# Scheduling a layer-norm, convolution and graph layer by stated latencies: pieces that name their time behind them, separate streams for rows and finishes

## The chip, the cores and the metric

One core of a Trainium2 chip. The metric is the device time of one execution in microseconds (us): the median of the runs, lower is better. The runs of one kernel differ by up to 0.55%, most of them by less. The experiments were taken on three chips, with the kernel before beside them each time (medians 2696.2 to 2699.8), so small differences between experiments are safer read from the ratios. A ratio is computed as the mean time of one kernel's fast runs over that of the other's of the same rounds, so it is not quite the ratio of the medians quoted.

## The reference

32 batches of a 512 x 256 matrix. A layer norm and relu give `h`. Three things are made from `h` and meet in a GRU-like gate:

```python
h = jnp.maximum(layernorm(x), 0.0)                  # per batch 512 x 256
# 1: convolution branch (channels first)
c = relu(bn1(conv1d(h, conv1_w, pad 0)))            # "rows" below: a 1-tap convolution
c = bn2(conv1d(c, conv2_w, pad 8))                  # 17 taps
x_conv = relu(c + h)
# 2: graph branch
s = h @ w_se.T + b_se                               # 3 columns
A = exp(-(squared distances of s)) * adj            # 512 x 512, from memory
x_nmp = A @ relu(h @ w_msg.T + b_msg)
# 3: gates
gi = concat(x_conv, x_nmp) @ w_ih.T + b_ih
gh = h @ w_hh.T + b_hh
r, z = sigmoid(gi_r + gh_r), sigmoid(gi_z + gh_z)
out = x + (1 - z) * tanh(gi_n + r * gh_n) + z * h
```

All arithmetic is f32.

## The kernel before

Batches go in groups of four. The 17-tap convolution is done by a nested fast algorithm: 25 products a group (called taps in places), whose input combinations ("operands") and output combinations ("sums") are VectorE and ScalarE work. An evacuation is the operation of another engine that reads a finished sum out of its buffer in PSUM, where TensorE writes its sums, and so frees the buffer. The kernel's author writes the issue order by hand: Python generators yield between pieces of TensorE work, and a loop decides which generator goes on. What is issued on one engine runs there in that order.

The pieces of one batch (cut):

```python
def begin(b):                       # transpose the normalized x: h
    for d in range(ND):
        norm_t(b, d)
        yield 0.55                  # TensorE us of the piece just issued
    if b + 2 < B:
        load(b + 2)                 # x_sb has two buffers
        NORMS[b + 2] = norm(b + 2)  # statistics: VectorE, issued bit by bit by pace()

def rows(b): ...                    # conv1: two pieces of 1.73
def graph(b):                       # messages, factors, exp, masks, gather
    for c in range(NT):
        messages(b, msg, c)
        if c == NT - 1:
            factors()               # VectorE
        yield 0.93
    factors_t(); yield 0.67
    kernel_exp(at); yield 1.2
    for n in range(NT):
        masked(b, at, n); yield 0.55
    for d in range(ND):
        yield from gather(b, msg, at, d)
```

The gates of a batch (cut); the last batch's finish (transposes of `o_sb`, whose last writer is GpSimd) stands inside them:

```python
for o in range(ND):
    yield from products(ps_r, o, 0, 0, 1)      # hidden part, 2 matmuls
    if o == 0:
        while b not in evacuated:
            SUMS.pop(0)[0]()                   # sums and xconv evacuations, ScalarE
        nc.vector.tensor_tensor(xconv, xconv, hT, op=ALU.add)
        nc.scalar.activation(xconv, xconv, AF.Relu)
        yield from finish_waiting()            # finish of the batch before
    yield from products(ps_r, o, 0, 1, 3)
    nc.scalar.activation(r, ps_r, AF.Sigmoid, ...)   # issued on the turn after the yield
    ...                                        # h, z, n likewise, then tanh and three GpSimd ops
```

The choice of the next generator goes by share of work done, and knows nothing of what is ready:

```python
def stage_one(g):
    for b in new:
        yield from begin(b)
        yield from graph(b)
    yield "rows wanted"             # convolution alone until the operands of the group are read
    for b in new:
        yield from rows(b)
...
streams["one"] = [stage_one(g + 1), 77.0 * 0.86, 0.0]
streams["three"] = [stage_three(g - 1), 130.0, 6.0]      # gates
streams["conv"] = [conv, 82.5 * 0.96, 0.0]
while streams:
    step(min(streams, key=lambda k: streams[k][2] / streams[k][1]))
```

Of the kernel before, what the change touches and what calls it, by code (L numbers as in the profile page):

```python
# [2 lines left out]

# [11 lines left out]
P = 128  # L15
# [10 lines left out]
_COL = {}  # L26
_NCOL = 0
for _n, _w in _VECS:
    _COL[_n] = _NCOL
    _NCOL += _w  # L30
G = 4
U = 57
V = U + 2
# [8 lines left out]
def kernel(  # L42
# [400 lines left out]
    def convolution():  # L443

        nonlocal at_product
        wg = (w for _ in range(NG) for w in weights_again())
        for g in range(NG):
            sums = summed(g)
            next(sums)
            done = None  # L450
            for n in range(25):
                at_product = m = 25 * g + n
                while len(WS) < min(m + 1 + AHEAD_W, 25 * NG):
                    WS.append(next(wg))
                while len(X2) < m + 1:
                    while operand_some() is None:
                        yield "rows", g
                w, x2 = WS[m], X2[m].rearrange("p (r v) -> p r v", v=V)
                ps = cps.tile([P, NZ], F32, name="ps_c")
                for o in range(ND):  # L460
                    matmul_sum(
                        ps[:, o * NU : (o + 1) * NU].rearrange("p (b u) -> p b u", u=U),
                        [
                            (w[:, k, i, o * P : (o + 1) * P], x2[:, i * G : (i + 1) * G, k : k + U])
                            for k in range(2)
                            for i in range(ND)
                        ],
                    )
                    if o == 0 and done is not None:
                        sums.send(done)  # L470
                    yield "pe", 1.65
                WS[m] = X2[m] = None
                done = ps
            sums.send(done)
            yield "group", g


    def late_pools():
# [89 lines left out]
            XR[b, c] = late.tile([P, 2, D], F32, name="y", bufs=2)  # L568
            nc.sync.dma_start(XR[b, c], x[b].rearrange("(c p) d -> p c d", p=P)[:, c : c + 2, :])

    waiting = []

    def finish_waiting():
        while waiting:
            for c in range(0, NT, 2):
                finish(*waiting[0], c)
                yield 0.55
            waiting.pop(0)

    def begin(b):  # L580

        for d in range(ND):
            norm_t(b, d)
            yield 0.55
        if b + 2 < B:
            load(b + 2)
            NORMS[b + 2] = norm(b + 2)

    def rows(b):
        nonlocal made  # L590
# [6 lines left out]
    def graph(b):  # L597

        msg = front.tile([P, NT, D], F32, name="msg", bufs=1)
        at = front.tile([P, NT, N], F32, name="at", bufs=1)  # L600
        for c in range(NT):
            messages(b, msg, c)
            if c == NT - 1:
                factors()
            yield 0.93
        factors_t()
        yield 0.67
        kernel_exp(at)
        yield 1.2
        for n in range(NT):  # L610
            masked(b, at, n)
            yield 0.55
        for d in range(ND):
            yield from gather(b, msg, at, d)

    def gates(b):
# [8 lines left out]
        def cols(o, g):  # L625
            return slice(g * D + o * P, g * D + (o + 1) * P)

        def products(ps, o, g, first, last):

            parts = [(whh, 0, hT[:, 0, :], hT[:, 1, :])]  # L630
            parts += [(wih, 0, *x_in[:2]), (wih, ND, *x_in[2:])] if x_in else [None, None]
            for k in range(first, last):
                w, at, *rhs = parts[k]
                for i in range(ND):
                    nc.tensor.matmul(  # L635
                        ps, w[:, at + i, cols(o, g)], rhs[i],
                        start=(k == first_of and i == 0), stop=(k == last_of and i == ND - 1),
                    )
                yield 1.73

        for o in range(ND):
            ps_r = acc.tile([P, N], F32, name="ps_acc")
            first_of, last_of = 0, 2
            yield from products(ps_r, o, 0, 0, 1)
            if o == 0:
                while b not in evacuated:
                    SUMS.pop(0)[0]()
                xconv = XC.pop(b)[:, :, :N]
                nc.vector.tensor_tensor(xconv, xconv, hT, op=ALU.add)  # L649
                nc.scalar.activation(xconv, xconv, AF.Relu)  # L650
                x_in = [xconv[:, i, :] for i in range(ND)] + [XN[b, d] for d in range(ND)]
                yield from finish_waiting()
            yield from products(ps_r, o, 0, 1, 3)
            r = late.tile([P, N], F32, name="r", bufs=2)
            nc.scalar.activation(r, ps_r, AF.Sigmoid, bias=brz[:, o : o + 1])  # L655
            ps_h = acc.tile([P, N], F32, name="ps_acc")
            first_of, last_of = 0, 0
            yield from products(ps_h, o, 2, 0, 1)

            nc.vector.scalar_tensor_tensor(  # L660
                r, ps_h, vec[:, _COL["b_hh"] + 2 * ND + o : _COL["b_hh"] + 2 * ND + o + 1], r,
                op0=ALU.add, op1=ALU.mult,
            )
            ps_z = acc.tile([P, N], F32, name="ps_acc")
            first_of, last_of = 0, 2
            yield from products(ps_z, o, 1, 0, 3)
            z = late.tile([P, N], F32, name="z")
            nc.scalar.activation(z, ps_z, AF.Sigmoid, bias=brz[:, ND + o : ND + o + 1])
            if o == 0:
                load_gates(b + 1)  # L670
            ps_n = acc.tile([P, N], F32, name="ps_acc")
            first_of, last_of = 1, 2
            yield from products(ps_n, o, 2, 1, 3)
            nc.vector.tensor_tensor(r, ps_n, r, op=ALU.add)  # L674
            nc.scalar.activation(  # L675
                r, r, AF.Tanh,
                bias=vec[:, _COL["b_ih"] + 2 * ND + o : _COL["b_ih"] + 2 * ND + o + 1],
            )

            t = o_sb[:, o, :]  # L680
            nc.gpsimd.tensor_tensor(t, hT[:, o, :], r, op=ALU.subtract)  # L681
            nc.gpsimd.tensor_tensor(t, z, t, op=ALU.mult)  # L682
            nc.gpsimd.tensor_tensor(t, r, t, op=ALU.add)  # L683
        load_res(b)
        load_sums(b + 1, 0)
        load_sums(b + 1, 1)
        waiting.append((b, o_sb))


    bn1_sc, bn1_sh = bn_affine("bn1")  # L690
# [40 lines left out]
                break  # L731
            credit -= 0.06 + 0.0011 * size

    def stage_one(g):

        new = range(g * G, (g + 1) * G)
        for b in new:
            yield from begin(b)
            yield from graph(b)
        yield "rows wanted"  # L740
        for b in new:
            yield from rows(b)

    def stage_one_first():


        def to_rows(b):
            yield from begin(b)
            yield from rows(b)

        yield from to_rows(0)
        for b in range(G):
            between = to_rows(b + 1) if b + 1 < G else iter(())
            for k, got in enumerate(graph(b)):
                yield got
                if k >= 3:
                    yield from islice(between, 1)

    def stage_three(g):
        for b in range(g * G, (g + 1) * G):  # L760
            yield from gates(b)

# [5 lines left out]
        for c in range(ND):  # L768
            nc.sync.dma_start(wflat[:, c, k0:k1, :], conv2_w[:, c, k0:k1, :])

    for got in stage_one_first():
        pace(got, 1.2)
    while prepare_next():
        pass

    conv = convolution()
    for g in range(NG):

        streams = {}
        if g + 1 < NG:  # L780
            streams["one"] = [stage_one(g + 1), 77.0 * 0.86, 0.0]
        if g > 0:
            streams["three"] = [stage_three(g - 1), 130.0, 6.0]
        streams["conv"] = [conv, 82.5 * 0.96, 0.0]
        rate = 0.4 if g > 0 else 0.7

        def step(name):

            stream = streams[name]
            got = next(stream[0], None)  # L790
            if got is None:
                del streams[name]
            elif got == "rows wanted":
                while freed < g:
                    step("conv")
            elif isinstance(got, tuple):
                kind, value = got
                if kind == "pe":
                    stream[2] += value
                    pace(value, rate)  # L800
                elif kind == "rows":
                    step("one")
                elif kind == "group":
                    del streams[name]
            else:
                stream[2] += got
                pace(got, rate)

        while streams:
            step(min(streams, key=lambda k: streams[k][2] / streams[k][1]))  # L810
    for got in stage_three(NG - 1):
        pace(got, 1.0)
    for _ in finish_waiting():
        pass


# [47 lines left out]
```

## Time and profile before

| | before |
|---|---|
| median, us | 2698.68 (2693.2 to 2703.8) |
| TensorE busy, granted clock | 89%, 0.935 |
| TensorE idle | 306 us |
| VectorE, ScalarE, GpSimd busy | 44%, 24%, 13% |
| DMA queue's share of 16 engines | 29.9% |

In the profile, L-numbers are lines of the kernel; "A <- B" in a wait is "A could not start until B ended". In a timeline row the two first numbers are start and length in us, and the bracket is the idle time of the engine just before. PE is TensorE, DVE VectorE, ACT ScalarE, POOL GpSimd, SPq the queue from which all DMA is issued. Of the names, `msg` and `aug` are the messages and the three columns of `s`, evacuated from one buffer; `augl` is made of `aug` for the factors; `veps` is a step of the layer norm's statistics; `y <- ps_tr` is the last addition of a finish.

### The profile page before, as it was taken

The numbers are of one execution on the slowest core, as the hardware profiler recorded it, in microseconds if no ns is written. First come the engines' busy times: TensorE is split into PE (matmuls) and PEld (weight loads), VectorE is DVE, ScalarE is ACT, GpSimd is POOL, SyncE is SP. The second block draws the span as 40 slices with busy tenths as digits, with TensorE's granted clock in tenths as the row PEclk, the third lists the DMA queues.
The fourth block names the chain that finished last, engine by engine and source line by source line (L and its number), as shares of the span: only waits on it lengthen the run. The fifth ranks groups of instructions, "written<-read, shape, count | busy, mean of one in ns | idle before, by whom it ended". The sixth has DMA issues, their size and how long they took to land.

```text
span 2695.4 us, 21705 instructions
## 1 busy us (share of the span) xinstructions
PE 2389.5 (89%) x8224; PEld 1493.0 (55%) x8224; DVE 1187.6 (44%) x1989; ACT 637.8 (24%) x930; POOL 337.4 (13%) x239
## 2 busy tenths in 40 slices
PE   5678878999799997999989998999979999999887
PEld 3347655655456654656556665555545565666443
DVE  5655625442455424554155443454435432544211
ACT  3322122222321213222132222322232221311211
POOL 1000001111011100111101101011101101121122
PEclk8779889999899998999999999999999999999899
DMA  5444333332233322333223332323223232232111
GB/s 206 171 144 152 121 118 102 117 106 90 67 113 110 110 101 77 111 109 110 87 77 106 117 117 71 105 102 110 102 74 113 94 108 76 79 114 88 55 63 31
DMA packets 132279, 277.87 MB, mean 103 GB/s; under 512 B 11984, under 2 KB 61520, under 8 KB 131536
## 3 DMA queue, kind: packets, MB, share of 16 engines
q1 hardware_dynamic: 132176, 276.50, 29.9%
q8 instruction: 65, 1.06, 0.2%
q14 instruction: 38, 0.31, 0.0%
HBM read 213.01 MB, written 63.44 MB: 103 GB/s over the span
## 4 chain that ended last, share of the span: by engine, by line
PE 78%; DVE 6%; ACT 4%; POOL 3%; issue 2%; DMA 1%; POOLq 0%; SPq 0%; DVEq 0%; ACTq 0%
PE ps_acc L635 36%; PE ps_c L92 21%; PE ps_g L545 8%; PE ps_g L92 7%; ACT xconv L412 2%; PE ps_tr L536 2%; POOL o_sb L681 1%; PE ps_tr L559 1%; PE ps_g L525 1%; PE ps_tr L217 1%; POOL o_sb L682 1%; DVE at L538 1%; DVE xconv L649 1%; POOL o_sb L683 1%; DMA x_sb<-in_x_dram 1%
## 5 line engine op out<-in xcount | busy, mean ns | idle before, releaser
L92 PE MATMUL ps_c<-x,w 128*128 128x228 f32 x3200 | 720.1, 370 | 45.1 <-issue 39.1
L92 PEld LDWEIGHTS ps_c<-x,w 128*128 128x128 f32 x3200 | 626.5, 199 | 209.5 <-issue 181.8
L635 PE MATMUL ps_acc<-xconv,wih 128*128 128x512 f32 x768 | 390.5, 634 | 40.7 <-ACT xconv L650 40.7
L635 PE MATMUL ps_acc<-hTb,whh 128*128 128x512 f32 x768 | 367.6, 607 | 25.9 <-ACT r L655 25.9
L635 PE MATMUL ps_acc<-xnb,wih 128*128 128x512 f32 x768 | 362.5, 594 | 0.0
L681 POOL TENSOR_TENSOR o_sb<-hTb,r 128x512 f32<-128x512 f32 x64 | 97.1, 1517 | 1575.8 <-ACT r L675 1575.8
L545 PE MATMUL ps_g<-at,msg 128*128 128x512 f32 x512 | 248.9, 614 | 21.4 <-DVE at L538 20.5
L635 PEld LDWEIGHTS ps_acc<-xconv,wih 128*128 128x128 f32 x768 | 153.0, 205 | 186.7 <-issue 140.6
L635 PEld LDWEIGHTS ps_acc<-hTb,whh 128*128 128x128 f32 x768 | 144.6, 193 | 155.5 <-issue 123.0
L635 PEld LDWEIGHTS ps_acc<-xnb,wih 128*128 128x128 f32 x768 | 144.9, 191 | 137.7 <-issue 136.4
L674 DVE TENSOR_TENSOR r<-ps_acc,r 128x512 f32<-128x512 f32 x64 | 44.1, 689 | 314.9 <-PE ps_acc L635 314.9
L545 PEld LDWEIGHTS ps_g<-at,msg 128*128 128x128 f32 x512 | 98.3, 195 | 123.0 <-issue 95.0
L238 DVE TENSOR_TENSOR x<-x 128x471 f32<-128x471 f32 x200 | 165.6, 839 | 0.6
L492 DVE TENSOR_TENSOR msg<-ps_g,bmsg 128x256 f32<-128x256 f32 x128 | 54.0, 423 | 249.2 <-PE ps_g L92 249.2
L538 DVE TENSOR_TENSOR at<-ps_tr,at 128x512 f32<-128x512 f32 x128 | 86.1, 687 | 170.6 <-PE ps_tr L536 170.5
L241 DVE SCALAR_TENSOR_TENSOR x<-x,x 128x471 f32<-128x471 f32 (+1 forms) x184 | 153.8, 836 | 2.3
L92 PE MATMUL ps_g<-wmsg,hT 128*128 128x259 f32 x512 | 139.8, 400 | 16.4 <-DVE aug L493 14.3
L551 ACT ACTIVATE xnmp<-ps_g 128x512 f32<-128x512 f32 x64 | 38.2, 597 | 454.1 <-PE ps_g L545 348.8
L559 PE MATMUL ps_tr<-ident,o_sb 128*128 128x128 f32 x256 | 53.9, 344 | 90.6 <-POOL o_sb L683 83.0
L147 POOL TENSOR_TENSOR rstd<-veps,mhalf 128x4 f32<-128x4 f32 x32 | 38.2, 1194 | 762.7 <-DVE veps L146 762.5
L92 PEld LDWEIGHTS ps_g<-wmsg,hT 128*128 128x128 f32 x512 | 99.1, 199 | 61.5 <-issue 44.4
L660 DVE SCALAR_TENSOR_TENSOR r<-ps_acc,vec,r 128x512 f32<-128x512 f32 x64 | 47.9, 748 | 192.8 <-PE ps_acc L635 192.8
(97 smaller groups left out, 2182.6 us busy)
## 6 DMA issues: line engine op xcount, KB each, us to landing
w<-wd SPq DMA_DIRECT2D x200, 512.0 KB, 3.5
m_sb<-in_adj_dram SPq DMA_DIRECT2D x128, 256.0 KB, 2.7
x_sb<-in_x_dram SPq DMA_DIRECT2D x32, 512.0 KB, 4.9
hd<-hT SPq DMA_DIRECT2D x32, 512.0 KB, 3.0
nd<-xnmp SPq DMA_DIRECT2D x64, 256.0 KB, 2.1
hTb<-hd SPq DMA_DIRECT2D x32, 512.0 KB, 4.1
xnb<-nd SPq DMA_DIRECT2D x64, 256.0 KB, 3.3
y<-in_x_dram SPq DMA_DIRECT2D x64, 256.0 KB, 4.0
```

The lines of the kernel that those rows point to most:

```text
L92: nc.tensor.matmul(ps, lhsT, rhs, start=(i == 0), stop=(i == len(pairs) - 1))
L238: nc.vector.tensor_tensor(dst, get(a), get(b), op=ALU.subtract)
L241: nc.vector.scalar_tensor_tensor(dst, a, -2.0, b, op0=ALU.mult, op1=ALU.add)
L412: nc.scalar.activation(XC[b][:, o, :].rearrange("p (u e f) -> p f e u", e=3, f=3), y[:, :, :, c : c + U], AF.Identity, bias=bn2_sh[:, o : ...
L492: nc.vector.tensor_tensor(msg[:, c, :], ps[:, :D], bmsg[:, :D], op=ALU.add)
L536: nc.tensor.transpose(ps[:, c, :], m[:, c * P : (c + 1) * P], ident)
L538: nc.vector.tensor_tensor(part, ps, part, op=ALU.mult)
L545: nc.tensor.matmul(ps, msg[:, c, d * P : (d + 1) * P], at[:, c, :], start=(c == 0), stop=(c == NT - 1))
L559: nc.tensor.transpose(ps[:, j, d * P : (d + 1) * P], o_sb[:, d, (c + j) * P : (c + j + 1) * P], ident)
L635: nc.tensor.matmul(ps, w[:, at + i, cols(o, g)], rhs[i], start=(k == first_of and i == 0), stop=(k == last_of and i == ND - 1),)
L660: nc.vector.scalar_tensor_tensor(r, ps_h, vec[:, _COL["b_hh"] + 2 * ND + o : _COL["b_hh"] + 2 * ND + o + 1], r, op0=ALU.add, op1=ALU.mult,)
L681: nc.gpsimd.tensor_tensor(t, hT[:, o, :], r, op=ALU.subtract)
```

## The change

The intent: let every piece say how long other engines need before its stream can go on, let the loop skip streams whose time has not come, make rows and finishes streams of their own, and issue each gate evacuation with the last matmul of its sum. No arithmetic, tile or buffer is altered. The core of the diff (cuts marked "...", comments added, the `if` lines before the last streams left out):

```diff
+    def run(streams, rate):
+        now = 0.0
+        ready = {name: 0.0 for name in streams}
+        hold = {name: HOLD.get(name) for name in streams}
+        while set(streams) - {"finish"}:
+            names = [k for k in streams if hold[k] is None or hold[k]()]
+            able = [k for k in names if ready[k] <= now]
+            if able:
+                name = min(able, key=lambda k: streams[k][2] / streams[k][1])
+            else:
+                name = min(names, key=lambda k: ready[k])
+                now = max(now, ready[name])
...
+                pe, after = got if isinstance(got, tuple) else (got, 0.0)
+                now += pe
+                ready[name] = now + after
...
             if c == NT - 1:
                 factors()
-            yield 0.93
+            yield 0.93, 0.0 if c < NT - 1 else 4.5
         factors_t()
-        yield 0.67
+        yield 0.67, 3.0
         kernel_exp(at)
-        yield 1.2
+        yield 1.2, 5.5
         for n in range(NT):
             masked(b, at, n)
-            yield 0.55
+            yield 0.55, 1.0 if n < NT - 1 else 2.5
...
+                if k == last - 1 and then is not None:
+                    then()                      # the evacuation, with the sum
+                yield 1.73, after               # 5.0 behind the residual
...
+    def all_finishes():
+        for b in range(B):
+            yield lambda: b in unfinished
+            yield 0.0, 10.0
+            for c in range(0, NT, 2):
+                finish(b, unfinished[b], c)
+                yield 0.55
...
+        streams = {"conv": [conv, 85.5 * 0.96, 0.0], "finish": [finishes, 1e9, 0.0]}
+            streams["graphs"] = [all_graphs(g + 1), 63.0 * 0.8, 0.0]
+            streams["rows"] = [all_rows(g + 1), 14.0, 9.0]
+            streams["gates"] = [all_gates(g - 1), 129.0, 6.0]
```

## The prediction

> **What bounds the kernel now.** I read the page first, then the engines' busy time by stage, then TensorE's waits in one repeating group, then its timeline at the start of that group. The page:
>
> ```profile
> PE 2389.5 (89%) x8224; PEld 1493.0 (55%) x8224; DVE 1187.6 (44%) x1989; ACT 637.8 (24%) x930; POOL 337.4 (13%) x239
> PE   5678878999799997999989998999979999999887
> PEclk8779889999899998999999999999999999999899
> PE 78%; DVE 6%; ACT 4%; POOL 3%; issue 2%; DMA 1%; POOLq 0%; SPq 0%; DVEq 0%; ACTq 0%
> ```
>
> TensorE is the only engine near full, and 78% of the chain that ended last is its work. But 89% is not 100%: 2695.4 - 2389.5 = 306 us idle, and the clock row falls under 9 where the busy row does. By stage (columns: window, its length, busy us of PE, PEld, DVE, ACT, POOL, granted clock, DMA share, GB/s):
>
> ```profile
> 0.00:172.00 172.00, 106.75 (x313) 55.98 (x313) 99.02 (x225) 60.60 (x108) 10.21 (x21) 0.79 0.50 184
> 172.00:366.50 194.50, 167.63 (x709) 127.63 (x709) 106.25 (x204) 39.47 (x68) 4.86 (x4) 0.92 0.40 137
> 1017.70:1338.70 321.00, 293.91 (x1029) 185.01 (x1029) 143.07 (x240) 78.80 (x112) 42.53 (x28) 0.95 0.29 100
> 2304.10:2541.00 236.90, 215.82 (x732) 140.81 (x732) 110.11 (x123) 40.87 (x52) 38.35 (x24) 0.95 0.25 85
> 2541.00:2695.00 154.00, 132.84 (x316) 60.63 (x316) 20.44 (x28) 26.21 (x33) 30.85 (x24) 0.93 0.16 51
> ```
>
> These are the startup, the first convolution group, one of six alike (366.5 to 2304.1 us in all), the last convolution group, and the gates left over. In the repeating group DVE, ACT and DMA are under half busy, so TensorE idles there on latency, not on another engine's throughput. Its waits in that group:
>
> ```profile
> PE ps_c L92 <- issue: 8.8, 3, 3.4
> PE ps_tr L559 <- POOL o_sb L683: 8.4, 3, 4.1
> PE ps_acc L635 <- ACT xconv L650: 5.2, 1, 5.2
> PE ps_acc L635 <- ACT r L655: 4.1, 1, 4.1
> PE ps_g L545 <- DVE at L538: 2.1, 2, 1.3
> ```
>
> (8.8 holds one 3.4 at each edge of the window; one belongs to the group, so the sum of all rows is about 27 us.) Four of these stand in the group's first 40 us:
>
> ```profile
> 1017.75 3.38 PE L92 MATMUL ps_c<-x,w 128*128 128x228 f32 x8 [3.37 <-issue]
> 1028.26 1.78 PE L92 MATMUL ps_c<-x,w 128*128 128x228 f32 x8 [2.02 <-issue]
> 1041.11 3.46 PE L635 MATMUL ps_acc<-xconv,wih 128*128 128x512 f32 x4 [5.18 <-ACT xconv L650]
> 1057.46 3.52 PE L635 MATMUL ps_acc<-hTb,whh 128*128 128x512 f32 x4 [4.12 <-ACT r L655]
> ```
>
> Each long gap is paid twice: after 3.4 us or more idle, eight records take 3.38 us and four take 3.46, where after the 2.02 us gap eight take 1.78.
>
> **The floor.** The trace has two records for each f32 matmul. In dense stretches of the timeline a piece of 4 convolution matmuls is followed 1.54 us later by the next (1070.07 to 1071.61), and two matmuls of 512 columns 1.72 us later. Counting the program's order (the same matmuls before and after): 1600 convolution matmuls x 0.386, 1536 of 512 columns x 0.86, 256 message matmuls x 0.44, 1184 transposes x 0.11, 128 small ones x 0.27 = 617 + 1321 + 113 + 130 + 35 = 2216 us. So 2695 holds 306 idle and some 173 of throttled clock (2695 x (1 - 0.935) = 175 agrees). A repeating group's floor is 277 of 321: 27 idle, 17 clock. Thus 1 us idle costs some 0.6 us more in clock.
>
> **What the Trainium skill says.** "TensorE: Matmul & The Clock Gate", section Part 1: the clock halves after an idle window of about 3.4 us and returns after a like time of sustained work. The doubled times above agree. "PSUM — Partial Sum Buffer", section Engine vs sequencer instructions: the queues of ScalarE, VectorE and GpSimd are strict FIFO; so where an evacuation is issued decides when it runs. The trace agrees: the sigmoid L655 stood behind a run of five xconv evacuations of 5.56 us. "ScalarE: Activation LUTs", section What ACT_TABLE_LOAD costs: about 1283 ns for a load and a drain besides; the trace shows 1283 ns for the load, and 48 of them; the new order has 50, so +2.6 us of ACT, off the path.
>
> **The change, part by part.** It alters no arithmetic, tile or buffer, only the order in which pieces are issued. I counted, in the new order, how much TensorE work (at the floor's rates) stands between a producer and its consumer.
>
> 1. *Finish as a stream.* The chain from the last gate matmul to the transposes is DVE 0.69 + ACT 0.72 + GpSimd 1.52 + 1.62 + 1.48 = 6.0 us. Before, 4.7 to 5.0 us of TensorE work (often nearer 2 in the gates' tail) covered it; now 9.6 to 10.7, and 5.2 in the tail. Gone: 8.4 us idle a group.
> 2. *Rows as a stream.* The eight-matmul run of the last rows no longer stands directly before the next group's first convolution tap: the last graph (exp, masks, gather, some 10 us) now stands between. The operand work (DVE 2.05 + 0.8) hides there: 3.4 + 2.0 us gone.
> 3. *Times behind pieces.* From first hidden product to the one on xconv there are now 4.4 to 5.7 us instead of 3.3 to 4.1, and evacuation starts two message pieces earlier: chain 2.35 + 1.23 + 1.06 = 4.6 us; the 5.2 us wait nearly goes. Messages to factor transposes: 4.6 to 6.7 us instead of 0.4 to 4.1; masks to gather 3.4 instead of 0 to 3.3; the short waits go.
> 4. *What stays.* At a group's start ACT still has eight evacuations in a row (8 x 1.28) with the relu of the residual inside; by my count the first sigmoid ends some 3 to 4 us after TensorE wants its buffer. Kept: 4 us.
> 5. *What is added.* Because graphs are held back, the fourth graph of every group ends alone: exp, masks and gather follow each other with 0 us between (before: 4.1 and 0 to 6.7). Four exps at about 0.5 us after a 1.28 table load, then four DVE multiplies at 0.65, against 1.76 us of mask transposes: some 4.2 us idle; two finishes before it hold both transpose buffers for another 1.6.
>
> New group: idle 4 + 4.2 + 1.6 + about 1.5 unnamed = 11, clock 11 x 0.6 = 7, so 277 + 18 = 295, and I take 297. Six groups: 1937.6 -> 1782.
>
> *Startup* (172 us): graphs 1 to 3 now have no filler at all, some 28 us each by the lone fourth graph of before (139 to 168 us); but begins and rows are done by about 70 us instead of 125, so 70 + 3 x 28 = 154; estimate 157. *First convolution group*: floor 150; its waits on aug, factors and masks (about 20 us) mostly go, an end like 5 stays: 172 instead of 194.5. *Last convolution group*: floor 204, the xconv wait (7.8) stays: 226 instead of 236.9. *Tail*: three finish waits of 3.9 become waits for the residual relu of about 1.7: 146 instead of 154. Sum: 157 + 172 + 1782 + 226 + 146 = 2483; with 7 us for what I have missed, **2490 us**, 7.7% less.
>
> **Rivals.** *The waits move instead of going* (parts 4 and 5): DVE is blocked in order while the new group's first sum waits for all evacuations, and DMA loads of x block it for up to 4.9 us after every begin. If the lone graph costs 10 us and the sigmoid 8, a group takes 310 and the whole some 2570. For: both are new or unmended in the order. Against: the mid-group distances all exceed their chains. *Startup loses*: graphs without filler at a clock near 0.75 could take 36 us each, +25 us. For: PEclk 7 in those slices already; against: rows made early let operand work start earlier. *Another engine becomes the bound*: DVE 143 of 297 us is 48%, ACT 27%, DMA 30%: I give it nothing. *Better than thought*: with gaps under 3.4 us the clock hardly drops; at 0.98, a group is 288 and the whole about 2430.
>
> **Range and chances.** The groups alone give 6 x (13 to 33) us, the ends -10 to +60: 2425 to 2570 should hold it 8 times in 10. For less than 2% (above 2645) three quarters of the gain would have to be lost: 0.04; slower 0.01; faster 0.95.
>
> **What would show it.** Right: finish transposes with no GpSimd wait outside the very end; convolution "issue" waits of 3.4 and 2.0 gone; group length 290 to 302 with a clock of 0.96 to 0.98. Part 4: one wait on the sigmoid of 3 to 4 us a group. Part 5: waits of masks on exp and of gather on the masks, once a group. Wrong: a group over 305, waits of TensorE on DVE in mid-group, or a startup over 175.

## The result

The changed kernel takes 2488.63 us (2486.51 to 2492.72, 4 runs) against 2700.12 for the kernel before in the same rounds: ratio 0.9221, 95% interval 0.9199 to 0.9244. From the page of the changed kernel, the rows that answer to those of before:

```profile
PE 2318.6 (93%) x8224; PEld 1449.6 (58%) x8224; DVE 1193.7 (48%) x1989; ACT 644.4 (26%) x932; POOL 329.0 (13%) x239
PE   5769979999899999999999998999989999999898
PEclk8779989999899999999999999999989999999899
```

Idle TensorE time went from 306 to 167 us (2485.4 - 2318.6), and throttled clock from 2695.4 x 0.065 = 175 to 2485.4 x 0.042 = 104 us: 139 + 71 = 210 us, the whole gain. By stage, in the columns of the prediction's table (window, length, busy us of each engine, clock, DMA):

```profile
0.00:158.60 158.60, 102.94 (x308) 53.46 (x308) 99.29 (x225) 59.54 (x107) 9.82 (x21) 0.79 0.54 200
158.60:351.40 192.80, 165.38 (x709) 126.32 (x710) 110.70 (x208) 41.01 (x69) 4.43 (x4) 0.90 0.39 134
645.60:941.50 295.90, 285.89 (x1029) 179.51 (x1028) 142.91 (x240) 79.48 (x112) 40.30 (x28) 0.98 0.34 109
2123.80:2341.60 217.80, 206.73 (x726) 134.06 (x724) 111.58 (x116) 42.67 (x54) 41.24 (x24) 0.98 0.29 93
2341.60:2485.40 143.80, 130.10 (x316) 58.52 (x316) 20.21 (x28) 26.35 (x33) 30.79 (x24) 0.95 0.17 55
```

| stage | before | predicted | after |
|---|---|---|---|
| startup | 172.0 | 157 | 158.6 |
| first convolution group | 194.5 | 172 | 192.8 |
| six groups alike | 1937.6 | 1782 | 1772.4 |
| last convolution group | 236.9 | 226 | 217.8 |
| gates left over | 154.0 | 146 | 143.8 |

The gain is where it was expected, in the six groups, but the first convolution group gained nothing. TensorE's waits in the repeating group (us in total, times, longest):

```profile
PE ps_c L93 <- issue: 3.7, 1, 3.7
PE ps_g L93 <- DVE aug L494: 1.8, 2, 1.6
PE ps_tr L537 <- ACT at L530: 1.6, 2, 1.3
PE ps_tr L512 <- DVE y L564: 0.9, 1, 0.9
PE ps_g L546 <- DVE at L539: 0.8, 1, 0.8
```

The finish, xconv and sigmoid waits are gone from the group. A convolution wait of 3.7 us is back, but at the third product and not at the group's first, in five of the six groups (18.3 us in all); and a message waits for `aug`. Over the whole run the finish waits, before and after, are

```profile
PE ps_tr L559 <- POOL o_sb L683: 83.0, 26, 5.4
PE ps_tr L560 <- POOL o_sb L675: 6.1, 2, 5.4
```

In the first convolution group it is the wait for `aug` which is large; there it is nearly all there is beside the weights' load:

```profile
PE ps_g L93 <- DVE aug L494: 19.6, 3, 7.7
PE ps_g L93 <- DVE veps L147: 5.7, 1, 5.7
PE ps_c L93 <- DMA w<-wd: 5.5, 1, 5.5
```

One occurrence, out of the timelines of the DMA queue, VectorE and TensorE:

```profile
164.33 0.38 SPq L100 DMA_DIRECT2D x_sb<-in_x_dram  x1
168.92 0.43 DVE L191 BATCH_NORM_STATS2 st<-x_sb 128x6 f32<-128x256 f32 x1 [21.88 <-DMA x_sb<-in_x_dram]
175.12 0.42 DVE L493 TENSOR_TENSOR msg<-ps_g,bmsg 128x256 f32<-128x256 f32 x1
175.75 2.06 PE L93 MATMUL ps_g<-wmsg,hT 128*128 128x259 f32 x4 [7.73 <-DVE aug L494]
```

The load of x two batches ahead is issued at 164.33, once TensorE has transposed the batch that held its buffer (161.84 to 163.20). The statistics that need it had been put into VectorE's queue ahead of the messages' evacuations, so VectorE stood from 147.04 to 168.92 with nothing else run in between: 17.3 us before the load was even issued, and 4.6 us of transfer. It then worked through statistics, normalization and an operand until 175.12, when the message's evacuation could run and free its PSUM buffer for TensorE. Over the whole run, in VectorE's waits of the kernel before:

```profile
DVE st L190 <- DMA x_sb<-in_x_dram: 62.6, 19, 9.8
```

and of the changed kernel:

```profile
DVE st L191 <- DMA x_sb<-in_x_dram: 250.6, 27, 21.9
```

So two questions were open: which parts of the change made the gain, and whether this wait for x is a real cost or a name for something else.

### The profile page after: what moved, and what is told of

The parts are those of the page before. It is cut to its first block, busy times and chain, and to the rows that moved or that the text cites. A ratio compares the mean times of both kernels' runs of the same rounds, so it can differ in the third digit from the quotient of the medians.

```text
span 2485.4 us, 21807 instructions
## 1 busy us (share of the span) xinstructions
PE 2318.6 (93%) x8224; PEld 1449.6 (58%) x8224; DVE 1193.7 (48%) x1989; ACT 644.4 (26%) x932; POOL 329.0 (13%) x239
## 5 line engine op out<-in xcount | busy, mean ns | idle before, releaser
L93 PE MATMUL ps_c<-x,w 128*128 128x228 f32 x3200 | 684.8, 359 | 24.0 <-issue 18.3
L93 PEld LDWEIGHTS ps_c<-x,w 128*128 128x128 f32 x3200 | 604.0, 191 | 149.7 <-issue 128.3
L634 PE MATMUL ps_acc<-xconv,wih 128*128 128x512 f32 x768 | 369.0, 603 | 13.7 <-ACT xconv L647 13.7
L634 PE MATMUL ps_acc<-hTb,whh 128*128 128x512 f32 x768 | 360.2, 595 | 5.4 <-DMA hTb<-hd 4.9
L546 PE MATMUL ps_g<-at,msg 128*128 128x512 f32 x512 | 255.8, 639 | 7.8 <-DVE at L539 7.8
L667 DVE TENSOR_TENSOR r<-ps_acc,r 128x512 f32<-128x512 f32 x64 | 44.2, 690 | 329.6 <-PE ps_acc L634 329.6
L93 PE MATMUL ps_g<-wmsg,hT 128*128 128x259 f32 x512 | 139.7, 403 | 46.9 <-DVE aug L494 38.4
L239 DVE TENSOR_TENSOR x<-x 128x471 f32<-128x471 f32 x200 | 179.8, 916 | 0.0
L191 DVE BATCH_NORM_STATS2 st<-x_sb 128x6 f32<-128x256 f32 x128 | 52.1, 407 | 250.6 <-DMA x_sb<-in_x_dram 250.6
L242 DVE SCALAR_TENSOR_TENSOR x<-x,x 128x471 f32<-128x471 f32 (+1 forms) x184 | 165.6, 900 | 2.6
L658 DVE SCALAR_TENSOR_TENSOR r<-ps_acc,vec,r 128x512 f32<-128x512 f32 x64 | 48.0, 750 | 208.4 <-PE ps_acc L634 186.1
L664 ACT ACTIVATE z<-ps_acc,brz 128x512 f32<-128x512 f32 x64 | 44.0, 687 | 311.9 <-PE ps_acc L634 311.8
L93 PE MATMUL ps_g<-hT,w 128*128 128x512 f32 x256 | 121.5, 608 | 1.0 <-ACT hT L219 1.0
```

Of the source, the lines that this page charges most:

```text
L93: nc.tensor.matmul(ps, lhsT, rhs, start=(i == 0), stop=(i == len(pairs) - 1))
L191: nc.vector.bn_stats(st[:, c, :], xs[:, c, :])
L239: nc.vector.tensor_tensor(dst, get(a), get(b), op=ALU.subtract)
L242: nc.vector.scalar_tensor_tensor(dst, a, -2.0, b, op0=ALU.mult, op1=ALU.add)
L546: nc.tensor.matmul(ps, msg[:, c, d * P : (d + 1) * P], at[:, c, :], start=(c == 0), stop=(c == NT - 1))
L634: nc.tensor.matmul(ps, w[:, at + i, cols(o, g)], hT[:, i, :] if k == 0 else x_in[2 * k - 2 + i], start=(k == of[0] and i == 0), stop=(k == ...
```

## The experiments

The theory: distance is what counts. A stated time puts enough TensorE work between a producer on another engine and its consumer; the other parts only make that possible. The rivals: the splitting into streams, or the early evacuations, do it. And for the first convolution group: the wait for x is a cost in VectorE's in-order queue, against the rival that another root only shows under that name. All kernels below gave correct results.

| run | what | median us | ratio to before (95%) |
|---|---|---|---|
| | the changed kernel | 2488.6 | 0.9221 (0.9199 to 0.9244) |
| e1 | no stated times at all | 2832.7 | 1.0505 (1.0483 to 1.0528) |
| e9 | only the finishes' time | 2610.6 | 0.9683 (0.9669 to 0.9697) |
| e5 | finishes held 4 us, not 10 | 2540.5 | 0.9420 (0.9397 to 0.9443) |
| e7 | rows not a stream | 2529.7 | 0.9374 (0.9358 to 0.9390) |
| e6 | gate evacuations late | 2467.3 | 0.9137 (0.9122 to 0.9152) |
| e2 | third x buffer | 2433.2 | 0.9022 (0.9007 to 0.9036) |
| e3 | statistics issued late | 2424.7 | 0.8981 (0.8961 to 0.9001) |
| e8 | e2 and e3 | 2425.7 | 0.8990 (0.8975 to 0.9005) |
| e4 | third x buffer, kernel before | 2664.2 | 0.9877 (0.9861 to 0.9892) |
| e10 | e3 and e6 | 2411.6 | 0.8947 (0.8933 to 0.8961) |
| e11 | e10, weights prepared later | 2428.3 | 0.9002 (0.8983 to 0.9020) |

### e1: no stated times

```diff
-                ready[name] = now + after
+                ready[name] = now
```

> The changed kernel, but every stream counts as ready at once: the times stated behind pieces are ignored (finishes, rows and early evacuations stay as they are). Theory A (the stated times make the gain): the finish transposes stand 0 us of TensorE work behind the last gate matmul, messages-to-factors and first-hidden-to-xconv distances shrink to 0 to 2.4 us, so TensorE's waits on GpSimd, xconv and factors come back, about 25 us idle a group or more, and the time is 2600 to 2720. Rival B (the splitting into streams and the early evacuations make the gain): 2480 to 2540.

Measured: 2832.7 us, slower than the kernel before. Theory A holds, and by more than its range: without its 10 us the finish, which has the highest priority, follows the last gate matmul at once, where the kernel before had 4.7 to 5.0 us between. TensorE's two largest waits in this run:

```profile
PE ps_tr L560 <- POOL o_sb L675: 178.0, 32, 7.0
PE ps_c L93 <- DVE x L239: 68.0, 8, 10.1
```

### e9: only the finishes' stated time

```diff
-                ready[name] = now + after
+                ready[name] = now + (after if name == "finish" else 0.0)
```

> The changed kernel with only the finishes' 10 us kept of all stated times. From the run without any stated times (2833 us, 178 us of finish waits on GpSimd) I take off those waits and 0.6 us of clock for each: 2833 - 285 = about 2550. Theory A (the other times, behind messages, factors, exps, masks and first hidden products, are worth some 60 us together): 2520 to 2600, with TensorE's waits on factors, xconv and convolution operands over 60 us in all. Rival B (only the finishes' time matters): 2480 to 2510.

Measured: 2610.6 us, Theory A, 10 us past the top of its range. The finish waits are gone (6.1 us left), but convolution operands cost as much as in e1 (68.0 and 37.7 us on the two `x` rows there):

```profile
PE ps_c L93 <- DVE x L239: 67.9, 8, 10.1
PE ps_g L93 <- DVE aug L494: 41.6, 8, 10.7
PE ps_c L93 <- DVE x L242: 35.5, 7, 5.8
```

So of the stated times, that of the finishes is worth 222 us when it alone is restored (2832.7 to 2610.6), the others 122 us more (2610.6 to 2488.6). A part of the first figure only repairs what the priority of the finishes breaks.

### e5: finishes as near as before

```diff
-            yield 0.0, 10.0
+            yield 0.0, 4.0
```

By the order of the built program, the finishes then have 3.9 to 5.0 us of TensorE work in front of them, as in the kernel before.

> The changed kernel with the finishes held back 4 us instead of 10: they then stand 3.9 to 5.0 us of TensorE work behind the last gate matmul (4.8 in the last convolution group, 1.7 in the tail), about as in the kernel before. Theory A (the distance of the finishes is what removed the GpSimd waits): waits of the finish transposes on GpSimd return to 60 to 110 us, and with the clock the time is 2540 to 2620. Rival B (they went because evacuations are issued earlier or because the queues are shorter): waits under 25 us, time under 2510.

Measured: 2540.5 us, at the low edge of Theory A's range, and the waits are back:

```profile
PE ps_tr L560 <- POOL o_sb L675: 71.3, 32, 5.4
```

The distance of the finishes is worth 52 us of the gain, net of what it shifts elsewhere: TensorE's waits on the sigmoid rise from 0.5 to 12.4 us, and its convolution waits fall from 18.3 to 1.6.

### e7: rows back at the end of the graphs

```diff
             yield from graph(b)
+        if g > 0:
+            yield lambda: freed >= g - 1
+            for b in range(g * G, (g + 1) * G):
+                yield from rows(b)
...
-            streams["graphs"] = [all_graphs(g + 1), 63.0 * 0.8, 0.0]
+            streams["graphs"] = [all_graphs(g + 1), 77.0 * 0.86, 0.0]
```

> The changed kernel with the rows of groups 1 to 7 back at the end of the graphs' stream instead of in their own. By order the rows then stand directly before the next group's first convolution tap, and the fourth graph no longer runs alone. Theory: the convolution waits of 3.4 and about 2 us return once a group with their clock loss, the lone graph's waits of about 3.7 us go, so the two nearly cancel: 2480 to 2520. If the rows' stream is a main part of the gain: over 2530.

Measured: 2529.7 us, 41 more than the changed kernel: past the range of the theory that the two effects nearly cancel, and at the edge of the other (over 2530). The convolution waits that came back were larger than reckoned:

```profile
PE ps_c L93 <- issue: 53.3, 16, 5.7
```

against 18.3 us in the changed kernel, and waits on `aug` rose from 38.4 to 52.1. The lone graph's waits on exp and masks fell as expected, from 12.7 and 7.8 us to 4.6 and 3.1. The lone graph that the rows' stream brings is a good exchange.

### e6: gate evacuations issued late again

```diff
-                if k == last - 1 and then is not None:
+                if k == last - 1 and then is residual:
                     then()
                 yield 1.73, after
+            if then is not None and then is not residual:
+                then()
```

> The changed kernel with the four evacuations of a gate half (reset, reset hidden, update, mix) issued after the piece's turn, as before, instead of with its last matmul; the residual stays early. If issuing them early matters by itself, TensorE waits on the sigmoid or on accumulator buffers return (over 15 us) and the time is 2510 to 2570; if the distances do the work, 2480 to 2505, within 1% of the changed kernel.

Measured: 2467.3 us, 21 us *faster* than the changed kernel; neither expectation. Issuing these four evacuations with their sum is not a part of the gain. TensorE's waits on the sigmoid did not return; its idle time in the profile is 152 us instead of 167. What fits is VectorE's queue: an evacuation placed with the matmul that feeds it makes VectorE stand until that matmul has run, and the waits of VectorE for accumulators (the two `r` operations) fall from 329.6 + 186.1 to 289.4 + 95.9 us. But its wait for the finish's transposes rises from 46.0 to 132.0 us, so a part of this is only waited elsewhere. On TensorE's side one thing stands out: the waits for a transpose buffer behind a finish's last addition (`DVE y L564`), 7.7 us in the changed kernel, are gone in e6, and 8.0 us of them go again from e3 to e10. So VectorE reaches those additions sooner. That this is the path of all 21 us was not isolated.

### e2 and e4: a third buffer for x, in both kernels

```diff
-        XS[b] = front.tile([P, NT, D], F32, name="x_sb", bufs=2)
+        XS[b] = front.tile([P, NT, D], F32, name="x_sb", bufs=3)
...
+                if b + 3 < B:
+                    load(b + 3)
                 if b + 2 < B:
-                    load(b + 2)
                     NORMS[b + 2] = norm(b + 2)
```

> The changed kernel with a third x buffer, each batch of x loaded one batch earlier, so that VectorE's statistics never stand in its queue before their data is there. Theory A (the change exposed a wait: VectorE is held 250 us by x loads in its in-order queue, and the 38 us of message waits, 9 us of veps waits and the 18 us of convolution waits follow from it): VectorE's idle time on x falls from 251 to under 30 us, TensorE's waits on aug from 38 to under 8 us, and the time falls by 40 to 80 us, to 2410 to 2450. Rival B (those waits have another root, such as the run of eight evacuations, and only change their name): 2470 to 2490.

> The kernel before with the third x buffer. Theory A (the wait for x became costly only through the change; before, VectorE was idle 63 us on x, most of it beside TensorE work): 2675 to 2705, under 1% gained. Rival (it cost as much before): 2620 to 2660.

Measured for the changed kernel with it: 2433.2 us, 55 less, within Theory A. VectorE's wait for x is

```profile
DVE st L191 <- DMA x_sb<-in_x_dram: 0.2, 1, 0.2
```

and TensorE's waits in the first convolution group, which had been 31 us, are 5.2 us on the weights' load and 2.0 on the rest. Waits on `aug` in the whole run fall from 38.4 to 13.4 us, of which 11.9 are one wait in the startup; the "under 8" that was expected left that one out. The convolution waits fell less, from 18.3 to 12.4. The wait for x is a cost by itself.

Measured for the kernel before with it: 2664.2 us, 35 less, between the two expectations. The wait was not harmless before. Most of it was gained by the end of the first convolution group: the group after it begins at 340.5 us instead of 366.5, 26 of the 35 us (2.6 of them in the startup). In that stage TensorE's waits on the factors fell from

```profile
PE ps_tr L511 <- DVE augl L506: 12.5, 4, 4.9
```

to

```profile
PE ps_tr L511 <- DVE augl L506: 4.7, 3, 2.2
```

So the change did not create the cost of waiting for x. By these two runs 35 us of it were there before, and the change, far from removing them, made it 55.

### e3 and e8: the statistics later in VectorE's queue

```diff
                     load(b + 2)
-                    NORMS[b + 2] = norm(b + 2)
+                    if b < G:
+                        NORMS[b + 2] = norm(b + 2)
...
+        if b >= G and b + 2 < B:
+            NORMS[b + 2] = norm(b + 2)
         factors_t()
```

> The changed kernel with two x buffers as it is, but from batch 4 on the statistics are issued after the messages of the same batch instead of before them. Theory A (as for the third buffer: it is the place in VectorE's queue, not the transfer, that costs): waits on aug under 12 us, time 2420 to 2460. If instead the transfer itself were late for its use, this would not help or hurt: 2480 to 2520.

> The changed kernel with the third x buffer and the statistics issued late, both at once. If the two act on the same wait, it adds nothing to the better of them (2425): 2415 to 2435; if the late load of x still costs something in the late version, 2395 to 2415.

Measured: 2424.7 us with two buffers, and 2425.7 with the third as well. Both are as the theory had it. With the statistics late, the buffer adds nothing and the transfer is in time (VectorE's wait for x is 1.9 us). The move also takes the statistics' own work out of the messages' way, so the 8.5 us by which e3 beats e2 need not come from the wait. Here a wait comes back that the prediction had kept and the changed kernel did not show:

```profile
PE ps_acc L637 <- ACT r L658: 8.6, 6, 1.6
```

once a group, at most 1.6 us: the sigmoid behind the run of evacuations. In e2 it did not come back (0.5 us in the whole run).

### e10 and e11: the best version, and a miss

e10 is e3 and e6 together. e11 adds this:

```diff
     def prepare_next():
+        if begun < 2:
+            return None
         return None if next(prepare, "done") == "done" else 700
```

> Statistics late (2425 us) and gate evacuations late (2467 us against 2489) together. If the two act on different waits, their gains add: 2400 to 2410. If the late evacuations only helped around the wait for x: 2420 to 2435.

> The same, with the preparation of the convolution weights held back until two batches have been begun, so that VectorE does not stand 8 us before the weights' arrival with the first messages behind it. If the startup hangs on that wait, its 9.1 us wait on aug goes and the first convolution starts 6 to 15 us earlier: 2385 to 2402; if the startup is bound by the preparation as a whole, nothing: within 5 us of the run beside it.

e10 measured 2411.6 us, 10.5% less than the kernel before and the best of all runs, but 2 us past the range for gains that add, and below that for gains that do not: neither expectation. Its gain over e3 is 13 us by the medians and 9 by the ratios to the kernel before, whose intervals touch (0.8961), where e6 alone had shown 21: the gains add only in part, and how far is near the noise. e11 measured 2428.3, 17 slower than e10; neither expectation had that (2385 to 2402, or within 5 us of e10). Its first convolution product begins at 171.1 us instead of 154.1, and its message wait of 8.6 us on `aug` is replaced by two:

```profile
PE ps_g L93 <- DVE aug L494: 10.4, 3, 7.8
PE ps_g L93 <- ACT at L530: 8.8, 1, 8.8
```

The startup does not hang on that one wait. Holding the preparation back moved all of it: ScalarE's first write of a prepared weight (`w <- gg`, L333) starts at 47.35 us instead of 32.91, and the last ends at 164.05 instead of 147.29, as much later as the first product. That fits a startup bound by the preparation as a whole; it was not tested by making the preparation shorter.

Not tested apart: the new shares of the streams, the new order of the startup, the 2 us behind a `begin`, and the early issue of the residual (it stays early in e6).

## Why the prediction was right, and where it was not

The total (2490 against 2488.6) is nearer than its terms, and that nearness is in part luck. The mechanism, distance between a producer and its consumer, is what e1, e9 and e5 bear out. The range was narrower than its own terms: groups 78 to 198 us and ends -10 to +60 make 2437 to 2627, where 2425 to 2570 was stated.

- **The floor and the clock.** Confirmed. The group's busy time fell to 286 us, near the floor of 277, at a clock of 0.98. Idle time again cost 0.62 us of clock for each us (104 over 167). But that only gaps of 3.4 us or more are paid twice was read from one group and is no rule. In the kernel before, eight records took 1.78 us after a gap of 3.37 at the start of another group, and in e2 three of five gaps of 2.48 us were followed by some 3.25 us:

```profile
366.48 1.78 PE L92 MATMUL ps_c<-x,w 128*128 128x228 f32 x8 [3.37 <-issue]
626.23 3.24 PE L93 MATMUL ps_c<-x,w 128*128 128x228 f32 x8 [2.48 <-issue]
```

- **Part 1, finishes.** Right: GpSimd waits fell from 83.0 to 6.1 us, 5.4 of them at the very end. The size was too large: 8.4 us a group with its clock, six times, and 8 in the tail make some 89 us, where e5, with the distances of before, costs 52: 65 us of finish waits returned (71.3 - 6.1), other waits fell, and the time rose by less than that.
- **Part 2, rows.** Right in kind: the waits of 3.4 and 2.0 us before the first taps are gone, and e7 returns the first (3.8 us a group). But one of 3.7 us came in their stead (below).
- **Part 3, times behind pieces.** Right for xconv in the groups (5.2 us to nothing). Wrong for the first convolution group: the step "its waits on aug, factors and masks (about 20 us) mostly go" failed for `aug`. The waits on factors and masks went (12.5 and 5.0 us to 0 and 0.8), but those on `aug` and `veps` grew from 2.1 and 1.6 us to 19.6 and 5.7. I took all of them for too little distance. The root of these was VectorE's wait for x, which no distance on TensorE mends; 172 became 192.8. e2 takes that stage to 158.7 us (159.2 to 317.9 in its trace), e4 shows the same root in the kernel before, there in a part of the factors' waits too. TensorE's waits on VectorE there (19.6 us on `aug`) are of the kind that the prediction named as a sign of being wrong. Its first rival names the x loads, but caps each block at 4.9 us, which on the page is the median from issue to landing. VectorE stood up to 9.8 us before the change and 21.9 after it, since the load itself waits for its buffer; and the sum gave them no time.
- **Part 4, the sigmoid wait.** The step "Kept: 4 us" failed in place. The 12.67 us that VectorE stood on x at a group's start (until 654.60 in the trace) delayed messages, evacuations, the residual and, behind the residual, a convolution operand. So TensorE stopped at the third tap for 3.7 us and at a message for 1.6, and by the time it reached the sigmoid's buffer that was free. With the statistics late (e3, e10) the third tap waits 0.8 us and the sigmoid wait returns, at 1.6 us at most. With the third buffer (e2), where VectorE doesn't stand on x either, the third tap still waits 2.5 us and the sigmoid doesn't. So the wait for x is not all of that gap. In e2's trace the operand still stands behind the residual's addition (ended at 623.41) and behind 1.2 us of the statistics' own work, and is ready at 626.13; in e3 the statistics are out of its way.
- **Part 5, the lone graph.** Right: the waits on exp, masks and finish buffers stand once a group, most of them at its end. They sum to 3.6 us (1.6 on exp, 0.8 of gather on the masks, 0.9 + 0.3 on finish buffers) where I had 5.8; 0.5 for a mask's load and 0.4 for the factors come on top.
- **Startup, last group, tail.** 157, 226 and 146 against 158.6, 217.8 and 143.8. The startup's graphs end at 153.1 us where 154 was reckoned; the 5.5 us behind them are a wait for the weights. In the tail the relu waits are 1.29 us, not 1.7; the xconv wait of the last group stayed, as was said, but with 9.9 us instead of 7.8.
- **The evacuations.** The prediction gave their early issue no time of its own. The four of a gate half have one: 21 us the wrong way.

So a miss of +21 us in one stage was offset by -10, -8 and -2 in three others (+2 in the startup), and of the 7 us set aside for what was missed 2 were used (the stages sum to 2485.4, the profiled span, against 2483). The first rival, waits that move, was half true: the x wait grew from 63 to 251 us of VectorE time and took 55 us that e2 gets back; but 35 us of that kind were there before (e4).

## What to carry to other kernels

When several streams share an in-order engine, state for each piece how long its consumers must wait, and let the scheduler put other work there: here this was worth more than 100 us beyond the finishes, and with no times at all the same streams were slower than the kernel before. Then look at what each *other* engine is made to stand at: an operation queued right behind its own load held everything behind it here, longest where the load itself waited for a buffer (17.3 of 21.9 us). Moving it later in the queue gained 64 us without a buffer (2488.6 to 2424.7). Issuing an evacuation as early as possible was not a gain by itself: it cost 21 us here, probably because it parks its engine in front of a matmul that has yet to run.

## What the Trainium skill lacked or had wrong

- "ScalarE: Activation LUTs", section What ACT_TABLE_LOAD costs: its 1283 ns for a load is what the traces show; its further drain of about 1380 ns for each switch is not seen. In the kernel before, a run of evacuations ended at 1055.40 us and the sigmoid behind a table load started at 1056.72, 1.32 us later for load and all.
- "PSUM — Partial Sum Buffer", section Engine vs sequencer instructions: it says that the queues are strict FIFO, and the runs agree. It lacks what this costs when the operation at the head waits for a DMA: 251 us of VectorE here, of which a third buffer gains 55 us of the whole, and another place in the queue 64.
- "TensorE: Matmul & The Clock Gate", section Part 1: its idle window of about 3.4 us agrees with most doubled times (3.38 us for eight records after a gap of 3.37), but does not tell from a single gap whether they come: after gaps of 2.48 us in e2 eight records took some 3.25 us three times of five, and after one of 3.37 in the kernel before they took 1.78.
